# Turned tiles of a graph-attention kernel: whole 128-column slots, and blocks moved inside SBUF by sixteen transfers in place of a trip through DRAM

## The chip, the core and the metric

The kernel runs on one core of a Trainium2 chip. The core has a matrix engine (TensorE, in the profile PE, with its weight loads as PEld), a vector engine (VectorE, DVE), an activation engine (ScalarE, ACT), a general engine (GpSimd, POOL) and a queue that issues the DMAs (SyncE, SP); sixteen DMA engines carry out what SP issues. The metric is the device time of one execution in microseconds, lower is better; the time of a kernel is the median of its runs.

## The reference

Input is `x`, 128 graphs of 128 nodes with 512 features in f32, one 128x128 matrix `adj`, and weights of 512x512. Two layers are computed for each graph:

```python
norm_adj = adj * deg_inv_sqrt[:, None] * deg_inv_sqrt[None, :]
h = relu(layernorm(x));  x = x + norm_adj @ (h @ W0) + b0            # layer 0: graph convolution
h = relu(layernorm(x))                                               # layer 1: attention, 8 heads of 64
q, k, v = h @ Wq + bq, h @ Wk + bk, h @ Wv + bv
scores = q k^T / 8 + (1 - adj) * -1e9
x = x + (softmax(scores) @ v) @ Wo + bo
```

## The kernel before

**Tiles and stages.** The 128 graphs are done in 32 groups `g` of four graphs `b`. A slot `t` of the main loop has five stages in the order W, Q, K, V, Y: W is the convolution's projection of group t+1, Q, K and V are those of group t, and Y is the output projection of group t-1. Each 512x512 projection is seven products in Winograd's scheme (`Projection`, steps 0 to 6), with sums of quarter matrices made beforehand (`combine`, on GpSimd mostly). The left operand of a projection lies in SBUF with features on the partitions, in 40 slots of 128 columns (`Operands`).

**The order is written by hand.** A table `plan` says ahead of which step of which stage a piece of side work stands: `at(t, "Q2b", f, ...)` puts `f` ahead of the second part of step Q2. Every engine then runs its instructions in exactly the order of the program. SP issues all DMAs in that order, too: a DMA that has to wait holds up all DMAs behind it. A DMA signals its end through one of eight semaphores taken in turn, and SP waits for the DMA that used the semaphore last before it issues the next one on it, so at most eight DMAs are under way.

**Turning a tile.** Two kinds of tiles have to be transposed: the normalised `h` of a group (it becomes the slots of `op_norm`) and the softmax weights `att` of a graph (128 queries x 8 heads x 128 keys). VectorE transposes 32x32 blocks in place of whole tiles, and the blocks are then moved by DMA.
- `flip_att(g, b)` (line 907): VectorE transposes the blocks of `att` into the fifth `att` buffer, called `spare` (512 KB), and SP writes `spare` to a DRAM tile `turned_b` (line 908).
- `turn_att(g, b)`: `from_dram` (line 797) reads it back into `att` with four DMAs of 128 KB in pieces of 1 KB.
- `flip_h(g, b)` (line 784): the same for `h`; graphs 0 and 1 fill `spare`, SP writes it to DRAM (line 786), graphs 2 and 3 fill `spare` again, and SP writes it again.
- `turn_h(g, half)`: four DMAs for each half bring it into `op_norm`.

A flip into `spare` has to wait until the DMA that reads `spare` is done. In the steady part of the loop the flips of one slot stand in the order att 0 (Q0b), att 1 (Q2b), att 2 (Q4b), att 3 (K0b), h 0 (K3), h 1 (K4b), h 2 (K6b), h 3 (V0b), and all use `spare`.

**What the pieces of 1 KB cost in layout.** The DRAM trip delivers a slot's 128 columns in four quarters of 32 that lie apart. `Operands("op_h", 4)` therefore keeps `op_norm` as [quarter][slot][32], and `halves` (line 149) takes such a slot as weights in four parts of 32 columns (the profile's 128*32) in place of two parts of 64 (128*64). `attend` (line 937) reads `att` in the same way.

**Around the change.** The stage V begins with `attend` for the last group, the `scores` of this group (matmuls at line 862, read by VectorE at line 869), and the first product of the values. `qs[g]` is a group's q (128 x 4 x 512), one buffer for all groups; it is written in Q and read last by `scores`. Line 490 is VectorE's addition of a bank to its tile, line 1122 the reload of a weight part, line 185 a load of `x`, line 955 a store of the output.

Of the kernel before, what the change touches and what calls it, by code (L numbers as in the profile page):

```python
# [8 lines left out]
F32 = mybir.dt.float32  # L9
# [39 lines left out]
SLOTS = 40  # L49
# [48 lines left out]
def kernel(  # L98
# [16 lines left out]
    nc = tc.nc  # L115
    B, N, D = x.shape
    P = 128
    H = 8
# [18 lines left out]
    def halves(out, lhsT, rhs, **flags):  # L137

        if len(rhs.shape) == 3:
            out = out.rearrange("p (q n) -> p q n", n=rhs.shape[-1])  # L140
        elif len(rhs.shape) == 4:
            out = out.rearrange("p (s q n) -> p s q n", s=rhs.shape[1], q=rhs.shape[2])
        if len(lhsT.shape) == 3:
            parts = [lhsT[:, q] for q in range(lhsT.shape[1])]
        else:
            parts = [lhsT[:, y : y + P // 2] for y in range(0, P, P // 2)]
        rows = P // len(parts)
        for y, part in enumerate(parts):
            nc.tensor.matmul(out[y * rows : (y + 1) * rows], part, rhs, **flags)  # L149

    def small_bank(name):
        return ps_t.tile([P, 512], F32, tag="bank", name=name)
# [10 lines left out]

    att_dram = [dp.tile([P, H * P], F32, tag=f"turned_{b}", name=f"turned_{b}") for b in range(GB)]
    h_dram = [dp.tile([P, H * P], F32, tag=f"turned_h_{y}", name=f"turned_h_{y}") for y in range(2)]
    spare = att_buf[GB].rearrange("p h k -> p (h k)")
    adj_sb, an = (att_buf[2][:, i, :] for i in range(2))
    bias_part = att_buf[4][:, 0:NC, :].rearrange("p c f -> p (c f)")  # L170
# [23 lines left out]
    class Weight:  # L194
        def __init__(self, t):
            self.t = t
# [188 lines left out]
    class Operands:  # L385


        def __init__(self, name, quarters=1):
            self.t = op.tile([P, SLOTS, P], F32, tag=name, name=name)
            whole = self.t.rearrange("p s n -> p (s n)")  # L390
            self.quarters = quarters
            self.cut = whole.rearrange("p (q s n) -> p q s n", q=quarters, s=SLOTS)

        def slots(self, some):
            return self.cut[:, :, some, :] if self.quarters > 1 else self.t[:, some, :]

        def blocks(self, i):
            return self.slots(slice(LEFT_AT[i], LEFT_AT[i] + 4))

        def slot(self, i, n):  # L400
            return self.slots(slot_of(True, i, n))

        def row(self, i, c):

            first = LEFT_AT[i] + 2 * c
            if self.quarters > 1:
                return self.slots(slice(first, first + 2)).rearrange("p q s n -> p s q n")
            return self.slots(slice(first, first + 2)).rearrange("p s n -> p (s n)")

        def fill(self, copy, b, src):  # L410

            half, j = divmod(b, 2)
            first = LEFT_AT[S1 if half else A11]
            dst = self.slots(slice(first + j, first + 8, 2))
            if self.quarters > 1:
                copy(dst.rearrange("p q c n -> p c q n"), src.rearrange("p (c q n) -> p c q n", c=NC, q=self.quarters))
            else:
                copy(dst, src.rearrange("p (c n) -> p c n", c=NC))

        def combine(self, engine, inner=True, then=None, within=None):  # L420

# [9 lines left out]
                    combine_one(within, self.slots, True, (A12, A22), step)  # L431


    op_mix, op_norm, op_att = (Operands(f"op_{k}", 4 if k == "h" else 1) for k in "aho")
    tail = []

    class Projection:
# [341 lines left out]
    def flip_h(g, b):  # L779

        half, j = divmod(b, 2)
        h2 = hs.pop((g, b)).rearrange("n (c i f) -> n c i f", c=NC, i=4)
        dst = spare.rearrange("n (i c j f) -> n i c j f", i=4, c=NC, j=2)[:, :, :, j, :]
        nc.vector.transpose(dst.rearrange("n i c f -> n c i f"), h2)  # L784
        if j:
            nc.sync.dma_start(h_dram[half], spare)

    def turn_h(g, half):
        op_h[g] = op_norm
        first = LEFT_AT[S1 if half else A11]  # L790
        from_dram(op_norm.slots(slice(first, first + 8)).rearrange("f q s n -> f q (s n)"), h_dram[half])

    def from_dram(dst, dram):

        for i in range(4):
            part = dram.rearrange("(q f) x -> f q x", q=4)[:, :, i * 256 : (i + 1) * 256]
            nc.sync.dma_start(dst[i * 32 : (i + 1) * 32], part)

    def attention_operands(g):
        op_h[g].combine(nc.vector if g < 1 else nc.gpsimd, g > 0, within=nc.gpsimd)  # L800
# [42 lines left out]
    def att_of(g, b):  # L843


        return att_buf[b]
# [57 lines left out]
    def flip_att(g, b):  # L904

        dst = spare.rearrange("q (i h k) -> q h i k", i=4, h=H)
        nc.vector.transpose(dst, att_of(g, b).rearrange("q h (i k) -> q h i k", i=4))  # L907
        nc.sync.dma_start(att_dram[b], spare)

    def turn_att(g, b):  # L910
        dst = att_of(g, b).rearrange("k h q -> k (h q)").rearrange("k (q x) -> k q x", q=4)
        from_dram(dst, att_dram[b])

    def transpose_att(g, b):
        att = att_of(g, b)
# [7 lines left out]
    def attend(g, b):  # L923
        if g not in op_o:
            op_o[g] = op_norm if g == NG - 1 else op_att
        aT = att_of(g, b)
        if not turned_in_place(g, b):
            aT = aT.rearrange("k h q -> k (h q)").rearrange("k (q h n) -> k h q n", q=4, h=H)
        if b == 2 or b == 3:
            po = small_bank(f"po_{g}_{b}")  # L930
        else:
            po = bank["b" if b == 0 else f"a{1 - turn[0]}"]
        for c in range(NC):
            for p in range(2):
                h = 2 * c + p
                out = po[p * HD : (p + 1) * HD, c * P : (c + 1) * P]
                nc.tensor.matmul(
                    out if turned_in_place(g, b) else out.rearrange("p (q n) -> p q n", q=4),
                    vs[g][:, b, h * HD : (h + 1) * HD],
                    aT[:, p * NC + c],  # L940
                    start=True,
                    stop=True,
                )
        op_o[g].fill(nc.scalar.copy, b, po)
# [20 lines left out]
    for t in range(-1, NG + 1):  # L965
# [3 lines left out]
        if 0 <= t - 1 < NG - 1:  # L969
            g = t - 1  # L970

            for first, final, place, f, *args in (
                ("W4", "Q0b", "Q0b", flip_att, 0),
                ("W6", "Q1b", "Q2", turn_att, 0),
                ("Q3", "Q2", "Q2b", flip_att, 1),
                ("Q5", "Q3b", "Q4", turn_att, 1),
                ("W6", "-Y3", "W2", exponentials, 2, 0, H // 2),
                ("Q1c", "-Y4", "W3", exponentials, 2, H // 2, H),
                ("Q4c", "-Y5b", "W4b", softmax_end, 2),
                ("Q6c", "-Y5", "W5", exponentials, 3, 0, H // 2),  # L980
                ("K0c", "-Y6", "W6", exponentials, 3, H // 2, H),
                ("K2c", "Q0b", "Q0b", softmax_end, 3),
                ("K1", "Q4", "Q4b", flip_att, 2),
                ("K3", "Q5b", "Q6", turn_att, 2),
                ("K3", "Q5", "K0b", flip_att, 3),
                ("K5", "Q5", "K2b", turn_att, 3),
            ):
                place = first if t == 1 else final if last else place
                if f in (flip_att, turn_att) and turned_in_place(g, args[0]):
                    continue  # L990
                at(t - place.startswith("-"), place.strip("-"), f, g, *args)
            if t == 1:
                at(1, "K3", transpose_att, g, 2)
                at(1, "K5", transpose_att, g, 3)
            elif last:
                at(t, "K1", transpose_att, g, 3)
            for b in (2, 3, 0, 1):
                at(t, "V0", attend, g, b)
# [15 lines left out]
        elif 1 <= t + 1 < NG and t >= 0:  # L1014
            g = t + 1
            at(t, "Q3b" if g < NG - 1 else "Q0b", ln2, g, 0)
            at(t, "K0b" if g < NG - 1 else "Q3b", ln2, g, 1)
            if g == NG - 1:

                places = ("Q3", "Q4", "Q5", "Q5", "Q6", "Q6", "K1", "K2", "K2")  # L1020
                steps = ((norm_h, 0), (norm_h, 1), (transpose_h, 0), (norm_h, 2), (transpose_h, 1), (norm_h, 3))
                steps += ((transpose_h, 2), (transpose_h, 3))
            else:
                places = ("K1c", "K2c", "K4c", "K5b", "K3", "K4b", "K6b", "V0b", "Y5")
                steps = ((norm_h, 0), (norm_h, 1), (norm_h, 2), (norm_h, 3))
                steps += tuple((flip_h, b) for b in range(GB))
                for half in range(2):
                    at(t, ("V6", "Y1b")[half], turn_h, g, half)
            for place, (f, b) in zip(places, steps):
                at(t, place, f, g, b)  # L1030
            at(t, places[8], attention_operands, g)
            at(t + 1, "Q3", attention_residual, g, 0)
            at(t + 1, "Q4", attention_residual, g, 1)
# [19 lines left out]
        if 0 <= t < NG:  # L1053
# [1 line left out]
            for b in (0, 1, 3, 2):  # L1055
                at(t, "V0", scores, g, b)
            if t > 0:
                at(t, "V0", output_operands, t - 1)
            at(t, "V1b", row_max, g, 0)
            at(t, "V3b", exponentials, g, 0, 0, H // 2)  # L1060
            at(t, "V4b", exponentials, g, 0, H // 2, H)
# [235 lines left out]
```

## Time and profile before

| what | value |
|---|---|
| median of 3 runs | 2553.16 us (2552.88 to 2561.6) |
| the profiled execution: its time | 2550.28 us |
| its span in the trace | 2548.4 us |
| TensorE busy, mean granted clock | 91% of the span, 0.96 |
| VectorE, GpSimd, ScalarE busy | 74%, 73%, 49% |
| DMA engines busy (SP's queue) | 68.6% of 16 engines |
| DMA packets, bytes | 261442, 596.19 MB |
| DMAs `turned<-att`, `att<-turned` | 121 of 512 KB, 484 of 128 KB |
| DMAs `turned_h<-att`, `op_h<-turned_h` | 58 of 512 KB, 232 of 128 KB |

The profile is of one execution, and its rows add up to that execution's span. A row of "waits" says which engine stood idle before which instruction, and what ended the idle time. The "chain" follows the work that ended last back from the end, at each step to what released it. One slot of the loop takes 78.57 us in the profiled execution (from a flip of att 0 to the next one).

### The profile page before, as it was taken

Reading aid. Unit: us, or ns where it says so; the run is one execution under the profiler, and the core shown is the slowest. Engines: PE = TensorE matmul, PEld = TensorE weight load, DVE = VectorE, ACT = ScalarE, POOL = GpSimd, SP = SyncE. Lnnn points to the kernel's source line nnn. Section 1 sums busy time; section 2 is a strip of 40 time slices with the busy share of each in tenths; the row PEclk is TensorE's granted clock in tenths of the full one; section 3 lists DMA queues with packets and bytes.
Section 4 is the critical chain, followed back from the end, with each engine's and each line's share of the span. In section 5 each row is a group of like instructions: output and inputs, shape, how many; then the busy total and the mean of one; then the engine's idle time right before and its main releaser. Section 6 shows DMA issues by size and latency. Waiting matters only on the chain.

```text
span 2548.4 us, 88607 instructions
## 1 busy us (share of the span) xinstructions
PE 2324.5 (91%) x36629; PEld 1909.2 (75%) x36629; DVE 1892.7 (74%) x4247; ACT 1249.0 (49%) x3823; POOL 1866.6 (73%) x1993
## 2 busy tenths in 40 slices
PE   9978898988999989999899998899998989889989
PEld 7767787777878778777777777777777877778777
DVE  6767787777877777777778777777767877778766
ACT  4645554454544545545455445454454544545443
POOL 7877777778677777677777777767778777787654
PEclk9989999999999999999999999999999999999999
DMA  5457767677777677676776767767777777767662
GB/s 184 166 205 239 266 224 262 228 235 251 246 253 258 220 245 252 231 253 220 241 272 224 258 225 235 255 226 256 233 233 250 243 251 243 234 239 249 222 233 96
DMA packets 261442, 596.19 MB, mean 234 GB/s; under 512 B 28208, under 2 KB 127152, under 8 KB 260528
## 3 DMA queue, kind: packets, MB, share of 16 engines
q1 hardware_dynamic: 261040, 590.53, 68.6%
q8 instruction: 289, 4.73, 0.8%
q14 instruction: 113, 0.93, 0.1%
HBM read 452.53 MB, written 137.89 MB: 232 GB/s over the span
## 4 chain that ended last, share of the span: by engine, by line
PE 55%; DMA 22%; DVE 16%; issue 3%; POOL 2%; ACT 1%; SPq 1%; DVEq 0%; POOLq 0%
PE bank_a L149 22%; PE bank_d L149 13%; DMA turned<-att 10%; PE bank_b L149 7%; PE bank_c L149 7%; DMA w<-wd_o 6%; DVE xt L490 5%; DMA turned_h<-att 5%; PE bank_d L862 3%; DVE att L907 3%; PE pa L149 2%; DVE xt L505 2%; DVE q L490 2%; DVE k L490 2%; DVE att L869 1%
## 5 line engine op out<-in xcount | busy, mean ns | idle before, releaser
L889 ACT ACTIVATE att<-att,nmx 128x128 f32<-128x128 f32 x1024 | 395.9, 391 | 205.0 <-DVE nmx L881 205.0
L902 POOL TENSOR_TENSOR att<-att,rsm 128x1024 f32<-128x1024 f32 x121 | 229.6, 1898 | 339.1 <-DVE rsm L896 232.3
L149 PE MATMUL bank_a<-op_h,w 128*64 128x256 f32 x2976 | 354.6, 380 | 0.0
L149 PE MATMUL bank_d<-op_h,w 128*64 128x128 f32 (+1 forms) x3424 | 226.7, 278 | 63.7 <-DVE q L490 63.7
L490 DVE TENSOR_TENSOR xt<-xt,bank_d 128x512 f32<-128x512 f32 x610 | 269.7, 467 | 11.9 <-PE bank_d L149 0.9
L149 PEld LDWEIGHTS bank_a<-op_h,w 128*64 128x64 f32 x2976 | 208.4, 138 | 82.7 <-issue 1.6
L149 PEld LDWEIGHTS bank_d<-op_h,w 128*64 128x64 f32 x3424 | 196.3, 138 | 77.6 <-DVE q L490 70.9
L833 ACT COPY v<-bank_a 128x512 f32<-128x512 f32 x96 | 56.3, 587 | 390.1 <-PE bank_a L149 352.5
L784 DVE STREAM_TRANSPOSE att<-h 128x512 f32<-128x512 f32 x116 | 81.8, 705 | 216.6 <-DMA turned_h<-att 211.3
L907 DVE STREAM_TRANSPOSE att<-att 128x1024 f32<-128x1024 f32 x121 | 150.3, 1242 | 109.1 <-DMA turned<-att 97.9
L862 PE MATMUL bank_d<-k,q 64*128 64x128 f32 x1024 | 114.6, 350 | 125.1 <-DVE att L869 124.3
L94 POOL TENSOR_TENSOR op_o<-op_o 128x256 f32<-128x256 f32 x297 | 212.8, 741 | 10.1
L149 PE MATMUL bank_a<-w,op_h 128*32 128x256 f32 x2976 | 213.0, 436 | 0.0
L819 ACT ACTIVATE q<-bank_a,bqk 128x256 f32<-128x256 f32 x192 | 80.0, 467 | 264.0 <-PE bank_a L149 263.8
L94 POOL TENSOR_TENSOR op_a<-op_a 128x256 f32<-128x256 f32 x279 | 197.6, 733 | 15.1 <-ACT v L833 5.4
L862 PEld LDWEIGHTS bank_d<-k,q 64*128 64x128 f32 x1024 | 96.2, 241 | 140.0 <-DVE att L869 132.2
L94 POOL TENSOR_TENSOR op_h<-op_h 128x256 f32<-128x256 f32 x270 | 190.9, 731 | 9.4
L889 ACT ACTIVATION_READ_ACCUMULATOR att<-att,nmx 128x1 f32 x1024 | 194.3, 190 | 0.0
L149 PE MATMUL bank_a<-w,op_o 128*64 128x256 f32 x1536 | 185.2, 383 | 0.0
L149 PE MATMUL bank_a<-w,op_a 128*64 128x256 f32 x1488 | 176.5, 379 | 0.0
L505 DVE TENSOR_TENSOR xt<-bank_a,xt 128x512 f32<-128x512 f32 x252 | 167.0, 683 | 3.1 <-PE bank_a L149 3.0
L149 PEld LDWEIGHTS bank_a<-w,op_h 128*32 128x32 f32 x2976 | 98.9, 125 | 78.8 <-issue 38.9
(197 smaller groups left out, 6038.4 us busy)
## 6 DMA issues: line engine op xcount, KB each, us to landing
w<-wd_v SPq DMA_DIRECT2D x155, 512.0 KB, 6.2
w<-wd_o SPq DMA_DIRECT2D x155, 512.0 KB, 10.2
w<-wd_q SPq DMA_DIRECT2D x150, 512.0 KB, 6.2
w<-wd SPq DMA_DIRECT2D x145, 512.0 KB, 5.2
turned<-att SPq DMA_DIRECT2D x121, 512.0 KB, 3.8
att<-turned SPq DMA_DIRECT2D x484, 128.0 KB, 3.0
out_dram<-xt SPq DMA_DIRECT2D x62, 512.0 KB, 4.6
turned_h<-att SPq DMA_DIRECT2D x58, 512.0 KB, 6.7
```

Of the source, the lines that this page charges most:

```text
L94: engine.tensor_tensor(twice(out), twice(x), twice(y), ALU.subtract if minus else ALU.add)
L149: nc.tensor.matmul(out[y * rows : (y + 1) * rows], part, rhs, **flags)
L490: nc.vector.tensor_tensor(dst, dst, src, f)
L505: nc.vector.tensor_tensor(t, src.rearrange("p (r f) -> p r f", r=2), t, ALU.add)
L784: nc.vector.transpose(dst.rearrange("n i c f -> n c i f"), h2)
L819: nc.scalar.activation(dst[:, r], src[:, r], AF.Identity, bias=bqk[:, i, oc : oc + 1], scale=1.0)
L833: nc.scalar.copy(dst, src)
L862: nc.tensor.matmul(pss[p][:, c, :], qs[g][rows, c, cols], ks[g][rows, c, cols], start=True, stop=True)
L869: nc.vector.scalar_tensor_tensor(dst, pss[p], SCALE, mask, ALU.mult, ALU.add)
L889: nc.scalar.activation(att[:, h, :], att[:, h, :], AF.Exp, bias=nmx[:, h : h + 1], scale=1.0, accum_out=sm[:, h : h + 1])
L902: engine.tensor_tensor(att, att, rsm.unsqueeze(2).to_broadcast([P, H, P]), ALU.mult)
L907: nc.vector.transpose(dst, att_of(g, b).rearrange("q h (i k) -> q h i k", i=4))
```

## The change

The DRAM tiles `turned_b` and `turned_h` go. After a flip the blocks are moved from the tile that holds them straight to the tile where they belong. A slot's 128 columns then lie side by side, which takes pieces of 32 columns (128 bytes), and one DMA can take only one range of partitions to another one, so each tile takes sixteen DMAs of 32 KB. `op_norm` loses its quarters, `halves` always takes two parts of 64 columns, and `attend` reads `att` plainly. The second half of `h` is flipped into the first half of `qs[g - 1]` (the q of the running slot) in place of `spare`. In `plan`, `turn_att` stands right behind its `flip_att`; the flips of h 2 and h 3 stand at V0b and V1b in place of K6b and V0b, and `output_operands` at V0c in place of V0.

```diff
-        if len(lhsT.shape) == 3:
-            parts = [lhsT[:, q] for q in range(lhsT.shape[1])]
-        else:
-            parts = [lhsT[:, y : y + P // 2] for y in range(0, P, P // 2)]
...
+        for y in range(0, P, P // 2):
+            nc.tensor.matmul(out[y : y + P // 2], lhsT[:, y : y + P // 2], rhs, **flags)
...
-    op_mix, op_norm, op_att = (Operands(f"op_{k}", 4 if k == "h" else 1) for k in "aho")
+    op_mix, op_norm, op_att = (Operands(f"op_{k}") for k in "aho")
...
-        dst = spare.rearrange("n (i c j f) -> n i c j f", i=4, c=NC, j=2)[:, :, :, j, :]
-        nc.vector.transpose(dst.rearrange("n i c f -> n c i f"), h2)
-        if j:
-            nc.sync.dma_start(h_dram[half], spare)
+        nc.vector.transpose(h_blocks(g, half).rearrange("n (i c j f) -> n j c i f", i=4, c=NC, j=2)[:, j], h2)
+
+    def h_blocks(g, half):
+        return qs[g - 1][:, 0:2, :].rearrange("p c n -> p (c n)") if half else spare
 
     def turn_h(g, half):
         op_h[g] = op_norm
         first = LEFT_AT[S1 if half else A11]
-        from_dram(op_norm.slots(slice(first, first + 8)).rearrange("f q s n -> f q (s n)"), h_dram[half])
-
-    def from_dram(dst, dram):
+        place_blocks(op_norm.t[:, first : first + 8, :], h_blocks(g, half))
+
+    def place_blocks(dst, src):
+        blocks = src.rearrange("p (i s n) -> p i s n", i=4, s=8)
         for i in range(4):
-            part = dram.rearrange("(q f) x -> f q x", q=4)[:, :, i * 256 : (i + 1) * 256]
-            nc.sync.dma_start(dst[i * 32 : (i + 1) * 32], part)
+            for y in range(4):
+                rows, cols = slice(i * 32, (i + 1) * 32), slice(y * 32, (y + 1) * 32)
+                nc.sync.dma_start(dst[rows, :, cols], blocks[cols, i])
...
         nc.vector.transpose(dst, att_of(g, b).rearrange("q h (i k) -> q h i k", i=4))
-        nc.sync.dma_start(att_dram[b], spare)
 
     def turn_att(g, b):
-        dst = att_of(g, b).rearrange("k h q -> k (h q)").rearrange("k (q x) -> k q x", q=4)
-        from_dram(dst, att_dram[b])
+        place_blocks(att_of(g, b), spare)
...
                 ("W4", "Q0b", "Q0b", flip_att, 0),
-                ("W6", "Q1b", "Q2", turn_att, 0),
+                ("W4", "Q0b", "Q0b", turn_att, 0),
                 ("Q3", "Q2", "Q2b", flip_att, 1),
-                ("Q5", "Q3b", "Q4", turn_att, 1),
+                ("Q3", "Q2", "Q2b", turn_att, 1),
...
-                ("K3", "Q5b", "Q6", turn_att, 2),
+                ("K1", "Q4", "Q4b", turn_att, 2),
                 ("K3", "Q5", "K0b", flip_att, 3),
-                ("K5", "Q5", "K2b", turn_att, 3),
+                ("K3", "Q5", "K0b", turn_att, 3),
...
-                places = ("K1c", "K2c", "K4c", "K5b", "K3", "K4b", "K6b", "V0b", "Y5")
+                places = ("K1c", "K2c", "K4c", "K5b", "K3", "K4b", "V0b", "V1b", "Y5")
...
-                at(t, "V0", output_operands, t - 1)
+                at(t, "V0c", output_operands, t - 1)
```

More of the change, by code (lines that the diff above doesn't have):

```diff
@@ L140, in halves @@
             out = out.rearrange("p (q n) -> p q n", n=rhs.shape[-1])
-        elif len(rhs.shape) == 4:
-            out = out.rearrange("p (s q n) -> p s q n", s=rhs.shape[1], q=rhs.shape[2])
-        if len(lhsT.shape) == 3:
-            parts = [lhsT[:, q] for q in range(lhsT.shape[1])]
-        else:
-            parts = [lhsT[:, y : y + P // 2] for y in range(0, P, P // 2)]
-        rows = P // len(parts)
-        for y, part in enumerate(parts):
-            nc.tensor.matmul(out[y * rows : (y + 1) * rows], part, rhs, **flags)
+        for y in range(0, P, P // 2):
+            nc.tensor.matmul(out[y : y + P // 2], lhsT[:, y : y + P // 2], rhs, **flags)
     def small_bank(name):
@@ L162 @@
     att_buf = [ap.tile([P, H, P], F32, tag=f"att{b}", name=f"att{b}") for b in range(GB + 1)]
-    att_dram = [dp.tile([P, H * P], F32, tag=f"turned_{b}", name=f"turned_{b}") for b in range(GB)]
-    h_dram = [dp.tile([P, H * P], F32, tag=f"turned_h_{y}", name=f"turned_h_{y}") for y in range(2)]
     spare = att_buf[GB].rearrange("p h k -> p (h k)")
@@ L385, with __init__ @@
     class Operands:
-        def __init__(self, name, quarters=1):
+        def __init__(self, name):
             self.t = op.tile([P, SLOTS, P], F32, tag=name, name=name)
-            whole = self.t.rearrange("p s n -> p (s n)")
-            self.quarters = quarters
-            self.cut = whole.rearrange("p (q s n) -> p q s n", q=quarters, s=SLOTS)
         def slots(self, some):
-            return self.cut[:, :, some, :] if self.quarters > 1 else self.t[:, some, :]
+            return self.t[:, some, :]
         def blocks(self, i):
@@ L400, in slot @@
         def slot(self, i, n):
-            return self.slots(slot_of(True, i, n))
+            return self.t[:, slot_of(True, i, n), :]
         def row(self, i, c):
             first = LEFT_AT[i] + 2 * c
-            if self.quarters > 1:
-                return self.slots(slice(first, first + 2)).rearrange("p q s n -> p s q n")
-            return self.slots(slice(first, first + 2)).rearrange("p s n -> p (s n)")
+            return self.t[:, first : first + 2, :].rearrange("p s n -> p (s n)")
         def fill(self, copy, b, src):
@@ L413, in fill @@
             first = LEFT_AT[S1 if half else A11]
[L414 to L418, printed above, removed]
+            copy(self.slots(slice(first + j, first + 8, 2)), src.rearrange("p (c n) -> p c n", c=NC))
         def combine(self, engine, inner=True, then=None, within=None):
@@ L926, in attend @@
         aT = att_of(g, b)
-        if not turned_in_place(g, b):
-            aT = aT.rearrange("k h q -> k (h q)").rearrange("k (q h n) -> k h q n", q=4, h=H)
         if b == 2 or b == 3:
@@ L935, in attend @@
                 h = 2 * c + p
-                out = po[p * HD : (p + 1) * HD, c * P : (c + 1) * P]
                 nc.tensor.matmul(
-                    out if turned_in_place(g, b) else out.rearrange("p (q n) -> p q n", q=4),
+                    po[p * HD : (p + 1) * HD, c * P : (c + 1) * P],
                     vs[g][:, b, h * HD : (h + 1) * HD],
-                    aT[:, p * NC + c],
+                    aT[:, p * NC + c, :],
                     start=True,
```

## The prediction

> **What bounds the kernel now.** I read the page first: its span and the chain of work that ended last, by engine and by line.
>
> ```profile
> span 2548.4 us, 88607 instructions
> ...
> PE 55%; DMA 22%; DVE 16%; issue 3%; POOL 2%; ACT 1%; SPq 1%; DVEq 0%; POOLq 0%
> ```
>
> Over half of the chain is TensorE, but 22% is DMA, and the page's list by line names `turned<-att` with 10% and `turned_h<-att` with 5%. These are the transfers that the change removes. So next the waits, longest in total first (engine, line, what it waited for: us in total, times, longest).
>
> ```profile
> DVE att L784 <- DMA turned_h<-att: 211.3, 29, 16.1
> ...
> PE bank_d L862 <- DVE att L869: 124.3, 29, 11.2
> ...
> DVE att L907 <- DMA turned<-att: 97.9, 80, 7.7
> ```
>
> VectorE waits before a flip because `spare` is still being read: 211.3/29 = 7.3 us in each slot for the third flip of `h`, and 97.9 us over all flips of `att`. The second row shows who waits for VectorE then: the scores' matmuls, 4.3 us in each slot. The chain of one slot, in order of time (start, us, what), shows both places.
>
> ```profile
> 1219.06 1.16 DVE att L907
> 1220.24 4.75 DMA turned<-att
> ...
> 1225.09 1.25 DVE att L907
> ...
> 1226.89 3.68 DMA turned<-att
> ...
> 1248.06 8.83 DMA turned_h<-att
> ...
> 1257.55 0.66 DVE att L869
> ...
> 1258.26 2.67 PE bank_d L862 x16
> 1260.93 3.53 PE bank_a L149 x32
> ```
>
> Flip, DMA, flip, DMA: the flips are a serial chain through `spare`. Over 28 steady slots the starts and ends of the flips in the trace give, from the end of flip att 0 to the start of flip h 0, 23.0 us on the mean (gaps of 4.8, 4.5, 4.6 and 5.3 us and three flips of 1.25 us); a slot takes 78.65 us. Of the gaps only 97.9/28 = 3.5 us in all is waiting, so `spare` is nearly, but not quite, free in time today. SP's timeline gives the price of issuing (start, us, DMAs).
>
> ```profile
> 1207.43 0.39 SPq L955 DMA_DIRECT2D out_dram<-xt  x1
> ...
> 1220.24 0.32 SPq L908 DMA_DIRECT2D turned<-att  x1
> ...
> 1225.04 1.74 SPq L797 DMA_DIRECT2D att<-turned  x4
> ```
>
> **How long `spare` is held after the change.** Now it is held for one DMA, 3.8 us in the median (page, issue to landing). Afterwards it is held until the last of sixteen DMAs has landed. Four issues of 128 pieces each fill 1.74 us, and their starts lie 0.47 us apart. Those ahead that found SP idle took 0.32 us with 128 pieces and 0.39 with 256; a new DMA has 32 partitions x 8 slots = 256 pieces. I take 0.49 us from start to start, so the last one starts 15 x 0.49 = 7.35 us after the first. For its landing I take 2.1 us: the 64 KB of `adj` landed in 1.8, the 128 KB read back from DRAM takes 2.4 at least (3.0 in the median). With 0.15 us for the two semaphore steps the hold is 9.6 us. Ends: 0.32 us (every issue as on an idle SP) gives 15 x 0.32 + 2.25 = 7.05 us; below that I have no row. At the other end the DMA engines set the pace. The trace's packets took 9 ns at 4 bytes, 27 at 512 bytes, 46 at 1 KB and 159 at 4 KB, a straight line on which 128 bytes cost 13 ns. A DMA has 256/16 = 16 pieces for each engine, 0.21 us, under the issue time. If a piece of 128 bytes cost as much as the 1 KB piece it replaces, it would be 16 x 46 = 0.74 us a DMA and the hold 15 x 0.74 + 2.25 = 13.3 us. The eight semaphores do not bind: the ninth DMA comes 8 x 0.49 = 3.9 us after the first, which has landed by then.
>
> The Trainium skill's page "DMA: Bandwidth & Descriptors" (Specifications) speaks against pieces this small: under 512 bytes a DMA engine is said to read, modify and write. As an estimate, a read and a write at 512-byte cost would make a piece 54 ns and the time about 3600 us. The 4-byte packets at 9 ns show no such penalty.
>
> **Engine time of the DMAs.** A turned tile costs 128 x 159/16 + 512 x 46/16 = 2.7 us of each engine now and 4096 x 13/16 = 3.3 us then; with six tiles a slot that is 4 us more in 78.65 us at 70% busy. I count nothing for it. What hides it is the idle 30%; without that cover it would be 4 us a slot.
>
> **SP.** A slot issues 6 x 5 DMAs less and 6 x 16 more; with 24 others that is 120 x 0.49 = 59 us of SP in a slot. SP does not become the bound of the slot. Behind each burst queue the weight parts (line 1122). The parts that matter stand at Y2 and Y3, behind the second burst of `h`: today they start at 1275.2, and they would start some 6 us later against TensorE and land about when step 3 of the next W uses them. I count 0, and up to 3 us a slot if they are late.
>
> **The chain of flips.** `turn_att` right behind its flip adds no wait of its own on SP, since it has to wait for that flip anyway. But flips att 1, 2, 3 and flip h 0 now each wait for the hold: 4 x 9.6 + 3 x 1.25 = 42.2 us in place of 23.0, so +19.2 us a slot. Behind the waiting flip on VectorE lie the readings of the banks (line 490), and TensorE stops soon after, as it does today for 2 us behind the flip at 1225. VectorE has only about 4 to 5 us of work between two flips, so the cover is used up.
>
> **The wait that goes.** Flip h 2 writes into q's buffer after the scores and waits for no DMA. TensorE's idle 4.3 us a slot goes, and with it the slow clock behind it. The windows show the granted clock in their last but two columns (start:end, length, busy times, clock, DMA share, GB/s).
>
> ```profile
> 1250.00:1252.20 2.20, 2.20 (x41) 2.03 (x38) 0.00 (x0) 1.36 (x3) 2.20 (x4) 1.00 0.99 305
> ...
> 1260.90:1262.50 1.60, 1.60 (x17) 0.75 (x20) 1.60 (x4) 0.00 (x0) 1.60 (x4) 0.50 0.00 0
> ```
>
> At half clock the scores take 2.67 us where the first took 1.16, and the product 3.53 where the same work later takes 1.73: 3 us more. Together -7.3 us a slot; the next thing late is TensorE itself, which is nearly gapless from there on. But the new waits before flip h 0 are about 4.6 us, again long enough for the clock to fall (an idle 2.15 us at 1225 did not lower it): +2.5 us in stage K, between 0 and 3. The ones before that fall into the next wait.
>
> **Weights of 64 columns.** In the rows by shape the values' products in four parts take as long as the output projection's in two (1.73 us a product, at full clock): 0. Reading `att` and `op_norm` plainly as the moving operand: 0, their matmuls take 275 ns in both forms. `output_operands` at V0c: 0, GpSimd is busy with `op_a` until then.
>
> **Sum.** +19.2 - 7.3 + 2.5 = +14.4 us a slot, 28 slots: +403 us. The last two slots have some flips without the rest: +20. 2550.28 (the profiled execution) + 423 = 2973, and 2.9 us more for the median: **2976 us**. A change under 0.5% (13 us) could not be told from none.
>
> **The rivals.**
> 1. The issues go at the pace of an idle SP: hold 7.05 us, chain 4 x 7.05 + 3.75 = 32 us, +9.0 - 7.3 + 0 to 2.5 = 1.7 to 4.2 a slot: 2610 to 2690, say 2650. For it: 0.30 to 0.32 us are real rows. Against it: all followers in a burst take 0.42 and more.
> 2. Faster: the wait removed at V0 outweighs the chain. This needs a hold under (23.0 + 7.3 - 3.75)/4 = 6.6 us, that is issues closer than 0.29 us. At 0.25 us the hold is 6.0 us, the chain 27.75 us, +4.8 - 7.3 = -2.5 a slot: 2480 us. For it: both waits on the DRAM write are on the chain today. Against it: no issue in the trace is that short. If the hold came out just at 6.6 us, nothing would change.
> 3. The pieces are dear: 46 ns each, hold 13.3 us, chain 57 us, +34 - 7.3 + 2.5 = +29.2 a slot, about 3390 us. For it: no piece of 128 bytes is in the trace. Against it: the line through four sizes.
> 4. The compiler of the program could still join the transfers of one tile, and then nothing of this holds; the four DMAs of a read are not joined today.
>
> **How the numbers follow.** Forecast 0.63 (2800 to 3150), rival 1 0.13, rival 2 0.09, rival 3 0.12, no change (the hold at 6.6, or rival 4) 0.03. Faster 0.09, same 0.03, slower 0.88. The range 2640 to 3350 leaves out rival 2, no change and about half of rival 3.
>
> **What would show it.** Right: 1936 DMAs into `att` from the spare tile and 928 into `op_h`, each 32 KB, starts about half a microsecond apart; packets near 900 thousand; VectorE waiting before L907 and L784 for these DMAs some 600 us in all, and no longer in V; the wait of L862 nearly gone; the clock at half in K. Wrong: starts under 0.3 us apart or flips that do not wait (rival 2), or DMA engines busy over 90% with landings of 5 us and more (rival 3), or a new wait of TensorE for weights in W.

## The result, and the profile after

The changed kernel takes 3544.14 us (median, 3539.89 to 3547.69) against 2553.11: 1.387 times as long, interval 1.3836 to 1.3903. A slot of the loop takes 112.6 us in place of 78.65. The page of the changed kernel first: span, SP's DMA queue (packets, MB, share of 16 engines), the chain by engine, and the row of the new transfers (count, KB each, us from issue to landing).

```profile
span 3540.0 us, 81122 instructions
...
q1 hardware_dynamic: 911168, 496.81, 48.8%
...
SPq 37%; PE 29%; DMA 23%; issue 5%; DVE 4%; POOL 1%; ACT 0%; DVEq 0%; POOLq 0%; ACTq 0%
...
att<-att SPq DMA_DIRECT2D x1936, 32.0 KB, 2.0
```

The DMA engines are less busy than before (48.8% against 68.6%), and a transfer lands 2.0 us after its issue. What leads the chain now is `SPq`, the time SP needs to issue: 37% against 1%. The waits name the flips again, now for the moves themselves, and a wait that was not there:

```profile
DVE att L892 <- DMA att<-att: 867.9, 90, 14.7
...
DVE att L765 <- DMA att<-att: 217.0, 28, 8.5
...
PE bank_b L142 <- DMA w<-wd: 170.9, 29, 6.9
```

L892 is the flip of att, L765 that of h (only h 0 waits now), and bank_b is the third product of stage W, for whose weights TensorE waits 5.9 us in each slot. The chain of the flips, from the end of flip att 0 to the start of flip h 0, grew from 23.0 to 55.9 us (gaps of 14.1, 12.6, 12.8 and 12.7 us). The first gap is the longest because the burst of att 0 stands behind large DMAs, some of which still hold one of the eight semaphores (a wait of SP's queue: us in total, times, longest):

```profile
SPq L782 <- DMA w<-wd_v: 33.9, 28, 2.0
```

The rest of the slot grew from 55.7 to 56.7, although the 7.3 us before flip h 2 are gone. SP's timeline (start, us, DMAs) shows why the rest did not shrink:

```profile
1726.32 11.35 SPq L782 DMA_DIRECT2D op_h<-att  x16
1738.06 0.33 SPq L1102 DMA_DIRECT2D w<-wd  x1
1738.56 11.71 SPq L782 DMA_DIRECT2D op_h<-q  x16
1750.32 1.55 SPq L1102 DMA_DIRECT2D w<-wd  x3
...
1766.20 11.40 SPq L782 DMA_DIRECT2D att<-att  x16
```

Sixteen issues take 11.4 us, some 0.7 each; from the first issue to the last landing, the tile that an att burst empties is held for 12.6 us in the median. The weight parts of W stand behind the second burst of h and go out at 1750.3; TensorE waits for them, and after the next flip for VectorE (the brackets: idle time before, and what ended it):

```profile
1754.66 0.69 PE L142 MATMUL bank_b<-w,op_a 128*64 128x128 f32 x4 [6.22 <-DMA w<-wd]
...
1755.57 3.62 PE L142 MATMUL bank_a<-w,op_a 128*64 128x256 f32 x16
...
1761.09 1.89 PE L142 MATMUL bank_a<-w,op_a 128*64 128x256 f32 x16
...
1781.29 3.26 PE L142 MATMUL bank_d<-op_h,w 128*64 128x128 f32 x28 [10.27 <-DVE q L472]
```

### The profile page after: what moved, and what is told of

It reads as the page before. It is cut to its first block, busy times and chain, and to the rows that moved or that the text cites. A ratio compares the mean times of both kernels' runs of the same rounds, so it can differ in the third digit from the quotient of the medians.

```text
span 3540.0 us, 81122 instructions
## 1 busy us (share of the span) xinstructions
PE 2524.6 (71%) x31605; PEld 2085.2 (59%) x31605; DVE 1898.5 (54%) x4247; ACT 1254.7 (35%) x3823; POOL 1864.9 (53%) x1993
## 3 DMA queue, kind: packets, MB, share of 16 engines
q1 hardware_dynamic: 911168, 496.81, 48.8%
## 4 chain that ended last, share of the span: by engine, by line
SPq 37%; PE 29%; DMA 23%; issue 5%; DVE 4%; POOL 1%; ACT 0%; DVEq 0%; POOLq 0%; ACTq 0%
SPq L782 35%; PE bank_a L142 11%; DMA w<-wd_v 10%; DMA att<-att 7%; DMA out_dram<-xt 6%; PE bank_d L142 5%; PE bank_b L142 3%; PE bank_c L142 3%; DVE att L892 2%; PE bank_d L847 2%; PE po L917 2%; SPq L1102 2%; PE pss L847 1%; PE bank_b L917 1%; DVE q L472 1%
## 5 line engine op out<-in xcount | busy, mean ns | idle before, releaser
L892 DVE STREAM_TRANSPOSE att<-att 128x1024 f32<-128x1024 f32 x121 | 150.5, 1244 | 868.0 <-DMA att<-att 867.9
L142 PE MATMUL bank_a<-op_h,w 128*64 128x256 f32 x2976 | 471.8, 474 | 0.0
L142 PE MATMUL bank_c<-op_h,w 128*64 128x128 f32 (+1 forms) x1712 | 176.8, 351 | 292.3 <-DVE q L472 174.8
L142 PEld LDWEIGHTS bank_a<-op_h,w 128*64 128x64 f32 x2976 | 263.4, 175 | 136.1 <-issue 84.4
L142 PEld LDWEIGHTS bank_c<-op_h,w 128*64 128x64 f32 x1712 | 137.1, 182 | 307.9 <-DVE q L472 182.0
L142 PE MATMUL bank_b<-op_h,w 128*64 128x128 f32 (+1 forms) x1712 | 147.9, 306 | 188.4 <-DVE q L472 188.4
L804 ACT ACTIVATE k<-bank_a,bqk 128x256 f32<-128x256 f32 x130 | 54.6, 471 | 583.0 <-PE bank_a L142 583.0
L142 PEld LDWEIGHTS bank_b<-op_h,w 128*64 128x64 f32 x1712 | 116.5, 155 | 219.7 <-DVE q L472 195.6
L142 PE MATMUL bank_a<-w,op_a 128*64 128x256 f32 x1488 | 220.3, 449 | 0.0
L142 PE MATMUL bank_b<-w,op_a 128*64 128x128 f32 (+1 forms) x900 | 83.1, 307 | 170.9 <-DMA w<-wd 170.9
L472 DVE TENSOR_TENSOR xt<-xt,bank_b 128x256 f32<-128x256 f32 x244 | 99.8, 409 | 189.1 <-PE bank_b L142 187.2
```

What stands on the lines that cost most here:

```text
L142: nc.tensor.matmul(out[y : y + P // 2], lhsT[:, y : y + P // 2], rhs, **flags)
L472: nc.vector.tensor_tensor(dst, dst, src, f)
L804: nc.scalar.activation(dst[:, r], src[:, r], AF.Identity, bias=bqk[:, i, oc : oc + 1], scale=1.0)
```

## The experiments

Each ran beside the kernel before on one chip, but not all on the same chip, so the ratios and not the times are compared between runs. "Chain" is the mean time from the end of flip att 0 to the start of flip h 0, "rest" the remainder of a slot; both are taken from the flips' starts and ends in each trace, for 27 or 28 steady slots.

| run | time, us | ratio to before (interval) | slot | chain | rest |
|---|---|---|---|---|---|
| before | 2553 | 1 | 78.7 | 23.0 | 55.7 |
| changed | 3544 | 1.387 (1.3836 to 1.3903) | 112.6 | 55.9 | 56.7 |
| half of h in q alone | 2374 | 0.9285 (0.9255 to 0.9314) | 72.9 | 23.3 | 49.5 |
| 1 KB pieces | 3477 | 1.3621 (1.358 to 1.3663) | 110.2 | 53.9 | 56.3 |
| 32 DMAs a tile | 5331 (one run) | 2.09 | 172.8 | 95.6 | 77.3 |
| two issuing engines | 3118 | 1.2217 (1.2183 to 1.225) | 98.0 | 38.8 | 59.1 |
| second burst of h later | 3516 | 1.3861 (1.3827 to 1.3894) | 111.6 | 62.8 | 48.8 |
| half of h in q, att 1 in k | 2368 | 0.9346 (0.9321 to 0.9371) | 72.5 | 22.8 | 49.7 |
| bursts of h by ScalarE | 3860 | 1.5106 (1.4998 to 1.5215) | 123.4 | 54.3 | 69.1 |
| att alone in SBUF | 3228 | 1.2655 (1.2557 to 1.2753) | 101.7 | 52.6 | 49.2 |
| h alone in SBUF | 2644 | 1.0364 (1.0281 to 1.0448) | 82.3 | 26.3 | 56.0 |

The theory at the start: a move lasts as long as its issuing engine needs for sixteen DMAs, and the flips wait for it one after the other. Its rival: the 128-byte pieces are what the DMA engines cannot carry fast enough.

**One part alone: the second half of h in q.** The DRAM trip and the quarters stay.

```diff
+        nc.vector.transpose(h_blocks(g, half).rearrange(...)[:, j], h2)
         if j:
-            nc.sync.dma_start(h_dram[half], spare)
+            nc.sync.dma_start(h_dram[half], h_blocks(g, half))
...
-                places = (..., "K4b", "K6b", "V0b", "Y5")
+                places = (..., "K4b", "V0b", "V1b", "Y5")
```

> The kernel before with one part of the change alone: the second half of h is flipped into q's buffer (flips at V0b and V1b), and everything still goes through DRAM with the quartered layout. My step 'the wait that goes' says that VectorE's 211 us before L784 vanish, that the scores' matmuls no longer wait (124 us) and that the clock stays up behind them: 7.3 us a slot, about 2340 us. The rival: the gain is given back where weights or operands come late, because V and Y then start 7 us earlier against the DMA queue (as TensorE's wait for w<-wd of 171 us in the changed kernel suggests); then 2480 us or more, with a new wait of PE for w or of POOL for op_h.

2373.64 us, 7% faster than before, though less than the 2340 expected: a slot is 5.8 us shorter, not 7.3. The longest wait of TensorE is now the one behind the flips of att, and the scores' wait is gone:

```profile
PE bank_d L149 <- DVE q L490: 66.5, 30, 3.6
```

The rest of a slot falls by 6.2 us. So this part of the change is a gain, and the others cost more than the whole difference.

**Larger pieces.** Sixteen DMAs of 32 pieces of 1 KB; the quarters stay.

```diff
-                nc.sync.dma_start(dst[rows, :, cols], blocks[cols, i])
+                nc.sync.dma_start(dst[rows, y], blocks[cols, i])     # 256 columns in one piece
```

> The changed kernel's way (sixteen DMAs from SBUF to SBUF, its schedule, h's second half in q), but with the quartered layout kept, so that each DMA has 32 pieces of 1 KB in place of 256 of 128 bytes. Theory (SP's time to issue a DMA grows with its pieces: 0.65 us apart at 256 pieces, 0.47 at 128): starts 0.35 to 0.45 us apart, hold of the spare tile 15 x 0.4 + 2.1 = 8.1 us, chain of the flips 36 us in place of 55.9: about 2950 us, less if the late weights of W go too. Rival (the price is per DMA, whatever its pieces): starts 0.65 us apart and about 3540 us.

3477 us: with an eighth of the pieces, issues still start 0.63 us apart (0.65 before), the chain is 53.9. That answers the question of the pieces: their number and size hardly matter. My own form of the theory, a price that grows with the pieces, falls as well; the price is per DMA. VectorE's wait before the flips of att is little shorter than the 867.9 us of the changed kernel:

```profile
DVE att L908 <- DMA att<-att: 825.4, 90, 14.4
```

**Thirty-two DMAs of half the size.**

```diff
-                nc.sync.dma_start(dst[rows, :, cols], blocks[cols, i])
+                for z in (slice(0, 4), slice(4, 8)):
+                    nc.sync.dma_start(dst[rows, z, cols], blocks[cols, i, z])
```

> The changed kernel with each of the sixteen DMAs cut into two of 128 pieces of 128 bytes. If SP's price is fixed per DMA (0.65 us): hold 31 x 0.65 + 2.1 = 22 us, 10 us more for each of four holds, about 4700 us. If it goes with the pieces alone (0.33 us for 128): no change, 3540 us. If it is a fixed part and a part per piece (0.45 to 0.47 us, as the 128-piece DMAs of the kernel before): hold 16.5 us, about 4060 us.

5331 us, above the dearest case named. Issues start 0.64 us apart with half the pieces. The chain grows by 39.7 us for 64 more issues (0.62 each), and the rest by 20.5 us for the 32 more issues of h (0.64 each). The second figure was not foreseen: the bursts of h lie on the path, issue for issue.

**Two issuing engines.** Every second DMA of a tile is issued by ScalarE.

```diff
-                nc.sync.dma_start(dst[rows, :, cols], blocks[cols, i])
+                queue = nc.scalar if y % 2 else nc.sync
+                queue.dma_start(dst[rows, :, cols], blocks[cols, i])
```

> The changed kernel with every second one of the sixteen DMAs issued by ScalarE in place of SyncE; the same pieces on the same sixteen DMA engines. Theory (the issuing sequencer sets the pace of a move): eight issues on each queue, hold about 7 x 0.65 + 2.1 = 6.7 us, chain of the flips about 31 to 33 us in place of 55.9, and the weights of W come earlier too: 2800 to 2950 us. Rival (the DMA engines' work on 128-byte pieces, or the eight semaphores in turn, sets the pace): holds of 11 us and more, 3400 to 3550 us. ScalarE's wait for the flip holds its other work up, which can cost some of the gain.

3118 us: same pieces, same DMA engines, and a hold of 7.9 us in the median in place of 12.6. The DMA engines do not set the pace; the issuing engine does. Nor do the eight semaphores inside a burst of the changed kernel: the ninth DMA is issued 8 x 0.65 = 5.2 us after the first, which lands after 2.0. The time falls short of the 2800 to 2950 expected, since ScalarE now has its own share of the chain (ACTq). The chain, and VectorE's wait before the flips of att:

```profile
PE 41%; DMA 21%; ACTq 13%; DVE 9%; ACT 7%; issue 5%; SPq 3%; POOL 1%; DVEq 0%; POOLq 0%
...
DVE att L893 <- DMA att<-att: 268.0, 59, 13.7
```

The Trainium skill's page "DMA: Bandwidth & Descriptors" (Issuing engines are not separate DMA queues) says that several issuing engines save only the time to initiate a DMA, usually small beside the DMA itself. The first half agrees; here the issues of one move took some five times as long as its last landing.

**The price of an issue by itself.** At the end of the kernel before, 4 or 8 DMAs of each of seven kinds in a row. L1263 is SBUF to SBUF in 8 x 32 pieces of 128 bytes, L1266 the same from DRAM (both below); L1258 is SBUF to SBUF over 128 partitions of 4 KB, L1260 over 32 partitions in one piece of 512 bytes, L1268 SBUF to DRAM and L1270 DRAM to SBUF with such pieces, L1272 SBUF to DRAM over 128 partitions of 1 KB.

```diff
+        for j in range(8):
+            part = flat[j // 4].rearrange("p (s n) -> p s n", s=8)[64:96, :, j % 4 * 32 : j % 4 * 32 + 32]
+            nc.sync.dma_start(part, spare[0:32, 0:256].rearrange("p (s n) -> p s n", s=8))
...
+            nc.sync.dma_start(part, att_dram[0][0:32, 0:256].rearrange("p (s n) -> p s n", s=8))
...
```

> The kernel before with DMAs added at its very end, of six kinds, 4 or 8 of each in a row, that do nothing for the result: SBUF to SBUF over 128 partitions (4 KB each), over 32 partitions in one piece of 512 bytes, and over 32 partitions in 8 pieces of 128 bytes as in the change; DRAM to SBUF over 32 partitions in 8 pieces of 128 bytes, and in one of 512 bytes; SBUF to DRAM over 32 partitions in one piece, and over 128. Theory (both sides in SBUF is what makes an issue dear): every SBUF-to-SBUF kind takes SP 0.5 to 0.65 us, even over 128 partitions, and every kind with DRAM on one side 0.3 to 0.45, even in 128-byte pieces. Rival (the small piece or the 32 partitions make it dear): the 128-byte kinds take 0.6 us with DRAM, too, and the 128-partition SBUF copy 0.3 to 0.45. The time itself should be that of the kernel before plus some 30 us.

2568 us in one run against 2538 on that chip, the 30 us expected. SP's timeline at the end (start, us for all of the kind, count):

```profile
2538.64 6.27 SPq L1260 DMA_DIRECT2D att<-att  x8
2544.95 5.24 SPq L1263 DMA_DIRECT2D att<-att  x8
2550.24 4.05 SPq L1266 DMA_DIRECT2D att<-turned  x8
2554.33 3.69 SPq L1268 DMA_DIRECT2D turned<-att  x8
2558.07 3.67 SPq L1270 DMA_DIRECT2D att<-turned  x8
2561.78 1.88 SPq L1272 DMA_DIRECT2D turned<-att  x4
```

With SBUF on both sides the issues start 0.65 us apart, with 512-byte pieces 0.63 (two of the eight at L1260 took 1.2 us, behind the 512 KB copies; the others 0.58 to 0.60). With DRAM on one side the same 256 pieces of 128 bytes go out every 0.49 us, larger ones every 0.46. So it is both sides in SBUF that makes an issue dear, and neither the pieces nor the 32 partitions. Nor is it the move to other partitions: in the changed kernel four of a tile's sixteen DMAs stay on theirs, and their issues last 0.61 us like the others (the first of a burst 0.59). The 128-partition copies between SBUF tiles say little, since 512 KB each fill the queue: 0.48 to 1.1 us.

**The weights ahead of the second burst of h.**

```diff
-                    at(t, ("V6", "Y1b")[half], turn_h, g, half)
+                    at(t, ("V6", "Y3b")[half], turn_h, g, half)
```

> The changed kernel with the second burst of h (sixteen DMAs) moved in SP's order from Y1b to Y3b, behind three of the weight parts that W waits for. Theory (behind the flips, the second loss is that W's weights are issued 10 us late, 171 us of TensorE's waiting for w<-wd): this wait goes, and GpSimd's later op_h costs less than it: 3370 to 3450 us. Rival (what W gains there, Q loses, because op_h is then ready later, or the flips' chain takes it up): within 1% of 3544 us.

The wait of bank_b for `w<-wd` is gone and the rest falls by 7.9 us, to 48.8; but the first gap of the chain grows from 14.1 to 21.3 us. On the mean SP starts the burst of att 0 3.5 us after the flip, in place of 0.1, and `spare` is held for 17.7 us, in place of 13.9, because the issues wait for large DMAs ahead of them that still hold one of the eight semaphores (waits of SP's queue):

```profile
SPq L782 <- DMA w<-wd_q: 94.7, 116, 2.1
...
SPq L782 <- DMA op_o<-in_x_dram: 58.7, 56, 2.6
```

The ratio, 1.3861, is that of the changed kernel. The rival was right: what W gains, the chain of the flips loses at the same queue.

**A second place for the flips of att**, on top of the faster run.

```diff
+        into = ks[g][:, 0:2, :].rearrange("p c n -> p (c n)") if b == 1 and g > 0 else spare
```

> The kernel before with the second half of h flipped into q's buffer (as the run of that part alone) and flip att 1 put into the first half of k's buffer, so that neither flip att 1 nor flip att 2 waits for a DRAM write. Theory (the flips' chain through the spare tile is still on the path): VectorE's 98 us before the flips fall to about 30, TensorE's 74 us before bank_d go, about 2310 to 2340 us against 2373. Rival (TensorE, 95% busy, has nothing left to gain there, and the chain goes over to the weights' DMAs): 2360 to 2380 us.

The ratio to before, 0.9346 (0.9321 to 0.9371), is not below that of the faster run; the gaps before flips att 1 and 2 fall to 3.2 and 3.3 us, and the third, before flip att 3, grows to 7.8. So VectorE's wait before the flips of att did not fall (112.8 us, 97.8 in the faster run), and TensorE's wait moved from bank_d (66.5 to 20.1 us) to bank_c (4.1 to 46.3). The rival's time was right. Its reason, that TensorE at 95% busy has nothing left to gain, is not shown by this run, since the wait only changed places.

**The bursts of h by ScalarE.**

```diff
-                nc.sync.dma_start(dst[rows, :, cols], blocks[cols, i])
+                queue.dma_start(dst[rows, :, cols], blocks[cols, i])      # nc.scalar for h, nc.sync for att
```

> The changed kernel with the two bursts of h (32 DMAs a slot) issued by ScalarE, and the bursts of att left on SyncE. Theory (outside the flips' chain, too, a slot waits for SP, which issues the bursts of h, then the weights, then the next att burst): TensorE's 171 us before bank_b for w<-wd go, the part of a slot outside the chain falls from 56.7 us to about 50, the chain stays at 55 to 56: about 3340 us. Rival (what is gained there is given back inside the chain, as when the second burst of h was only moved behind the weights): chain 61 us or more, 3500 us and more. ScalarE stands still while it issues, 21 us a slot, which may cost the exponentials some of the gain.

3860 us. The wait of bank_b for `w<-wd` is gone and the chain did not grow (54.3 us), so the rival's reason fails though its "3500 us and more" holds; the rest grew to 69.1 us, against the 50 expected. ScalarE stood in its order with the exponentials behind the bursts, and VectorE and GpSimd behind those:

```profile
DVE rsm L881 <- ACT att L874: 578.6, 31, 22.2
...
ACT att L874 <- DMA op_h<-att: 389.0, 28, 16.3
```

It moves the loss to other engines and does not settle what the bursts cost on SP. The next two runs take the question apart instead.

**Att alone, and h alone, in SBUF**, both with quarters and h's second half in q.

```diff
# att alone
-        nc.sync.dma_start(att_dram[b], spare)
-        from_dram(dst, att_dram[b])
+        place_quarters(dst, spare)          # sixteen DMAs of 32 KB
# h alone
-            nc.sync.dma_start(h_dram[half], h_blocks(g, half))
-        from_dram(..., h_dram[half])
+        place_quarters(..., h_blocks(g, half))
```

> The kernel of the faster run (DRAM trip, quartered layout, h's second half in q) with the att tiles alone moved inside SBUF by sixteen DMAs of 32 KB each, right behind their flips; h still goes through DRAM. Theory (two losses, of which the flips' chain is the larger): the chain grows from 23.3 us to about 53, as in the run with 1 KB pieces, and the rest of a slot stays at 49.5 to 51 us: a slot of 103 to 104 us, 3230 to 3270 us. Rival (the rest of the slot is late because of the att bursts, too): 56 us for the rest, 3420 us.

> The kernel of the faster run with the two halves of h alone moved inside SBUF by sixteen DMAs each; att still goes through DRAM, with one DMA out and four back. Theory: the chain of the flips stays near 23 to 24 us; the bursts of h hold SP for 20 us in V and Y, and the weights of W behind them come late, so the rest grows from 49.5 to about 56 us: a slot of 79 to 80 us, 2560 to 2590 us. Rival (the price of the bursts of h is only seen where the att bursts follow on SP): 2373 to 2400 us.

Att alone: 3228 us, the chain 52.6 and the rest 49.2, as the theory had it (the time just below its range). H alone: 2644 us, more than the 2590 expected; the rest grows to 56.0, and the chain by 3.0, its first gap being 7.5 us. The wait for W's weights is there without any burst of att:

```profile
PE bank_b L149 <- DMA w<-wd: 145.6, 29, 6.5
```

The parts add up. From the faster run's 72.9 us a slot, att costs 28.9 and h 9.4, together 111.2; the run with 1 KB pieces, which has both, takes 110.2.

## Why the prediction was wrong

The direction held, and so did the mechanism of the chain: the flips became a serial chain through `spare`, the issues and not the bytes set its pace, and VectorE waits there, 1085 us in both rows. The predicted slot was 14.4 us longer; it is 34.0 us longer. Of the 19.6 us that are missing, 13.7 lie in the chain and 5.9 in the rest of the slot.

- **The issue was priced at 0.49 us (main error).** That is what 256 pieces take with DRAM on one side, to the digit; all rows it came from had DRAM on one side. From SBUF to SBUF an issue takes 0.65, and 0.71 on the mean with a few of 0.9 to 1.9 us. The hold is 12.6 us in the median, not 9.6, and the chain grew by 32.9 us a slot, not 19.2; four holds that are 3.0 us longer make 12.0 of the 13.7. The upper end I had put on the hold, 13.3 us from rival 3, has the right size with the wrong reason: a piece of 128 bytes takes 12 ns in the packet records, and the straight line gave 13. No row of the trace before showed an SBUF-to-SBUF DMA, and I bounded the pieces, not that.
- **"SP does not become the bound of the slot", and 0 to 3 us for the late weights.** I added up SP's issues (59 us a slot) and found room. But SP works in order, and the two bursts of h stand ahead of the weights of W and of the next att burst. The second burst takes SP 11.7 us, not 7.8, and TensorE waits 5.9 us a slot for the weights: the prediction's own sign of being wrong, a new wait for weights in W. The product behind that wait takes 3.6 us in place of 1.9 in the slot shown above (clock 0.50, the last of the windows below). Together that is about the 7.2 us by which the rest is longer than in the faster run (56.7 against 49.5). H alone costs 9.4 us a slot, and twice the issues of h cost the rest 20.5 us more.
- **"The eight semaphores do not bind."** Inside a burst they do not. At the front of the burst of att 0 they do, since the DMAs ahead of it are of 512 KB and take longer to land; that is most of what the first gap has more than the others (14.1 against 12.6 to 12.8).
- **The wait that goes: -7.3.** Confirmed as a part: the rest fell by 6.2 us in the run of that part alone. The bursts of h took it back.
- **The slow clock in K: +2.5.** The clock does fall: to 0.50 behind flip att 3 (1695.7), inside the chain, and to 0.76 behind flip h 0 (1709.0), where I had placed the cost (windows of the changed kernel; the third column from the end holds the clock). Still, with att alone the rest is no longer than in the faster run (49.2 against 49.5), so no net cost shows outside the chain.

```profile
1699.00:1703.00 4.00, 3.67 (x20) 2.34 (x22) 2.42 (x8) 0.00 (x0) 3.90 (x5) 0.50 0.33 52
...
1709.00:1713.70 4.70, 3.45 (x28) 2.33 (x30) 4.41 (x13) 1.88 (x3) 4.51 (x7) 0.76 0.95 359
...
1754.60:1759.00 4.40, 4.34 (x26) 2.79 (x28) 2.26 (x6) 0.00 (x0) 4.16 (x6) 0.50 1.01 353
```

- **Weights of 64 columns, 0; landing, 2.1 us; DMA engine time, 0.** These held. The values' products of 128x256 take 381 ns in the rows by shape, as the output projection's (379); the landing is 1.96 us; the DMA engines were busy about as long as before (48.8% of 3540 us against 68.6% of 2548; the sum in the prediction gives 3.5 us more a slot, not 4). The rule that under 512 bytes an engine reads, modifies and writes (Trainium skill, "DMA: Bandwidth & Descriptors", Specifications) shows no cost here: 733 thousand packets of 128 bytes have a median of 12 ns. That its estimate, about 3600 us, lies near the measured time is a coincidence.

## What to carry to other kernels

Count DMAs, and price each by a row with the same memories on both sides; where none exists, the price of the issue is the open term, and not the bytes. A buffer that is emptied by one DMA is free when that lands, one that is emptied by sixteen is held for sixteen issues, so a trip through DRAM with one DMA out can be the faster way. And a queue that works in order can be on the path well before it is full (SP was issuing for 46% of the span with h alone in SBUF): look at what stands behind each burst. The gain here was the smaller step: the version with the second half of h in q alone beats both kernels, 2374 us, 0.9285 of the time before.

## What the runs showed of the hardware

- In a row, SP's issues of DMAs from SBUF to SBUF (32 partitions, 32 to 256 pieces, 128 bytes to 1 KB) start 0.63 to 0.65 us apart, and with DRAM on one side 0.43 to 0.49. Why is not shown.
- About one issue in 25 takes 0.9 to 1.9 us (78 of 1936 into `att`); no run tells the cause.
- Packets of 128 bytes took 12 ns of a DMA engine, on the line through 4 bytes, 512 bytes, 1 KB and 4 KB.
